# Slots, block experts and two expert loads moved around the seam between the second sequence and the expert blocks

## The chip, the cores and the metric

The kernel runs on one core of one Trainium2 chip. Its time is the device time of one execution in microseconds (us). A core has five instruction streams that run beside each other, each strictly in its own order and held up only by semaphores: PE (TensorE, matrix multiplication), DVE (VectorE), ACT (ScalarE), POOL (GpSimd) and SP (SyncE, which here only issues transfers). Transfers between the main memory and the on-chip memory (SBUF) run on 16 DMA engines; they are issued from SP, ACT or POOL. Results of PE go to eight PSUM banks.

## The reference

`x` has 8 sequences of 512 tokens with 512 channels. What is computed:

```python
xn = layernorm(x)
# attention, for each sequence, 16 heads of 32 channels
q, k, v = rotate(silu(xn @ Wq)), rotate(silu(xn @ Wk)), xn @ Wv
o = lightning_attention(q, k, v)          # decaying state, chunks of 128 tokens
o = o * sigmoid(xn @ Wg1 @ Wg2)
o = o * rsqrt(mean(o * o, per head) + 1e-6) * norm_weight
s = o @ Wo
# mixture of experts over all 4096 tokens, 16 experts, each token goes to its best 4
probs = softmax(xn @ gate_w.T)
weights, chosen = top_k(probs, 4)         # weights normalised to sum 1
mixed = sum of weights[e] * ((silu(xn @ Wg[e]) * (xn @ Wu[e])) @ Wd[e])
shared = the same with one expert for all, times sigmoid(xn @ shared_gate_w)
out = x + s * silu(mixed + shared)
```

## The kernel before

The work has three stages. **Stage one** (0 to about 316 us): all tokens are normalised, routed and run through the shared expert, the attention of sequences 0 and 1 is computed beside that, and the chosen (token, expert) pairs are sorted by expert into blocks of 128 rows. **Stage two** (to about 706 us): the expert blocks; 112 of them go as 56 pairs of one expert, the rest singly. **Stage three**: the attention of the other six sequences, and the mixture's sum, gathered per token. The change lies at the seam from stage one to stage two.

**The end of sequence 1** is the end of `sequence`, in its branch for `n == FIRST`. For each of four groups `g` of heads, `output` makes the output product `po`. Behind the last of them come: `gate_1` (the gate's first product `pg`), `squares` (the squares `sq` by ACT, their sums per head `pr` by PE, the root `rs` by ACT), `inverse` (the reciprocal of `rs` by DVE), the last quarter of the next sequence's `value` (`pv`), and `normed`: PE spreads `rs` over the channels (`pb`), and DVE multiplies it into `on`, in four instructions, one for each 128 tokens. Then `project` makes `on @ Wo` for each 128 tokens (`pw`, 8 matmuls each) and `spill` copies the result with ACT (`so`) and stores it (`s_d`).

**The table.** `table` finds which token stands at which place of which block. It is a generator: each `next(filling)` does one piece, here between the matmuls of sequence 1. It compares lists on DVE and ACT, and multiplies them on PE in four rounds of 16 matmuls (`pn`), added up by DVE in `acc`. After the last round PE folds the result (`pslot`) and DVE turns it into `slot`, the row numbers that the gathers use. The table's scratch memory is the room in `wexp` of the last `LATE` = 5 of the 16 experts. When it has been read, these experts' weights are loaded there, 768 KB each: three by SP when the last round begins (L556), the last two by ACT at the end (L1077), after `for _ in filling`, which runs the rest of the table behind everything in `sequence`.

**The block experts.** `experts_of_blocks` (six instructions by DVE, L1256 to L1263) works out from the ends of the experts' lists which expert each block belongs to, as offsets `eoff`. Its scratch is `xts`, a tile that takes the place of sequence 2's `xT`, so it waits for the last `pv`. Every block reads its weights at an offset from `eoff`, so the program cannot know which expert it touches: each read of `wexp` counts as a read of all of it, and waits for every load of `wexp` that was issued before it in the program.

**The pairs.** For each pair `j`: `gather` (POOL, two indirect DMAs that fetch the rows of 128 tokens by `slot`, into six homes, three in `xg` and three in `more`), `turn_rows` (SP, two DMA transposes of half of each row, `pl`), `transpose_x` (PE, the other half, `pt`), `join` (ACT copies `pt` and `pl` into `xts`; for pair 0 DVE copies `pl`), `prepare` (DVE copies the gate and up weights out of `wexp` into `wst`, then the routing weights `w`), `gate_up` (PE, 16 matmuls `pgu`; then `slb` by ACT and DVE), and `down` (PE, two matmuls `py` for each pair's two blocks, which read `wexp` itself; DVE scales them to `y`, SP stores `y_d`). `begin(0, ...)` starts the chain with pairs 0 and 1, with the gate's second product of sequence 2 (`gate_2`, `p` at L645, four sigmoids by ACT) between; `blocks` then goes through all pairs, turning pair j+2, preparing pair j+1 and gathering for pair j+4 around the products of pair j. `aside(j)` is a hook called in each round after `gate_up`.

**The order on an engine** is that of a scheduler which works on estimated times, except where the text pins it: `on_pe()` chains PE's instructions in program order, `behind(ENGINE)` puts an instruction behind the last one pinned on that engine, and `tc.issue_after(x)` puts one behind a given other. Four PSUM banks are called "a", two "d", one "k", one "m". The `tmp` tiles (`so`, `y`, `rs`, the gate's `g1`) share `TMP` buffers.

Of the kernel before, what the change touches and what calls it, by code (L numbers as in the profile page):

```python
# [12 lines left out]
I32 = mybir.dt.int32  # L13
U32 = mybir.dt.uint32
U16 = mybir.dt.uint16
# [19 lines left out]

NB = (B * N * TOPK + E * (P - 1)) // P
WE = KC * 2 * F + D
TMP = 4
FIRST = 2
NBQ = -(-NB // 4)  # L40

# [56 lines left out]
def tile_block(ctx: ExitStack, tc: tile.TileContext, a: dict, out: bass.AP):  # L98
# [384 lines left out]
    def table(room):  # L483
# [99 lines left out]
                    pt[h * HALF : (h + 1) * HALF, :NB], lhsT=fold,  # L583
                    rhs=acc.rearrange("p (b h) -> p b h", h=2)[:, :, h], start=True, stop=True)
        t = const.tile([P, NB], I32, tag="slot", name="slot")
        nc.vector.tensor_scalar(t, pt[:, :NB], float(B * N // 2), None, ALU.add)
        slots.append(t)


# [19 lines left out]
    def value(b, t):  # L609
        if t == 0:  # L610
            v_of[b] = att.tile([P, NC, D], F32, tag="v", name=f"v_{b}", bufs=2)
        pv = bank("d" if t % 2 else "m", f"pv_{b}_{t}")
        for k in range(KC):
            with on_pe():
                nc.tensor.matmul(  # L615
                    pv, lhsT=xT_of[b][:, k, t * P : (t + 1) * P], rhs=wv[:, k, :],
                    start=(k == 0), stop=(k == KC - 1))
            between[0]()
        nc.scalar.copy(v_of[b][:, t, :], pv)
# [4 lines left out]
    def gate_1(b):  # L624
        pg1 = bank("a", f"pg1_{b}")
        with on_pe():
            for k in range(KC):
                for t in range(NC):
                    nc.tensor.matmul(
                        pg1[t * Q : (t + 1) * Q, :P], lhsT=wg1[:, k, :],  # L630
                        rhs=xT_of[b][:, k, t * P : (t + 1) * P],
                        start=(k == 0), stop=(k == KC - 1))
        g1_of[b] = att.tile([P, P], F32, tag="tmp", name=f"g1_{b}", bufs=TMP)
        nc.scalar.copy(g1_of[b], pg1[:, :P])
# [156 lines left out]
    def inverse(b):  # L791
        nc.vector.reciprocal(rs_of[b], rs_of[b])

    def normed(b):
        pbs = [bank("a", f"pb_{b}_{c}") for c in range(NC)]
        rs = rs_of.pop(b)
        with on_pe():
            for g in range(G):
                for c in range(NC):
                    cq = slice(c * Q, c * Q + H)  # L800
                    nc.tensor.matmul(
                        pbs[c][:, g * C : (g + 1) * C], lhsT=wge[cq, g * P : (g + 1) * P],
                        rhs=rs[cq, :], start=True, stop=True)
        for c in range(NC):
            oc = on_of[b][:, :, c * C : (c + 1) * C]
            nc.vector.tensor_tensor(  # L806
                oc, oc, pbs[c].rearrange("p (g t) -> p g t", t=C), ALU.mult)

    def project(b, t):
        pw = bank("d", f"pw_{b}_{t}")  # L810
# [7 lines left out]
    def enter(b, step=lambda: None, ps=None):  # L818

        key(b, 0, ps)  # L820
        step()
        query(b, 0)
        step()
        key(b, 1)
        step()
        by_token(b, 0)
        query(b, 1)
        step()

    def sequence(b, step, projected, before=None, defer=False, also=lambda: None):  # L830


        n = b + 1

        def project_tiles(q, ts):
            if q is not None:
                for t in ts:
                    projected(q, t, project(q, t))


        fill = ([0], [1], [2], [3], [], [], [], [])
        for g in range(G):
            scores(b, g)
            step()
            if g + 2 < G:
                key(b, g + 2)
            else:
                value(n, 2 * (g - 2))
            if g + 1 < G:
                by_token(b, g + 1)  # L850
            project_tiles(before, fill[2 * g])
            step()
            if g + 2 < G:
                query(b, g + 2)
                if g + 3 == G and n not in xT_of:
                    load_xT(n)
            if g + 2 == G:
                value(n, 1)
            if g == 0 and b not in on_of:
                gate_2(b)  # L860
            project_tiles(before, fill[2 * g + 1])
            if fill[2 * g + 1] == [NC - 1]:
                on_of.pop(before, None)
            output(b, g)
            if defer and g + 2 == G:
                gate_1(n)
            step()
        v_of.pop(b)
        if n == FIRST:
            gate_1(n)  # L870
            squares(b)
            inverse(b)
            value(n, 3)
            normed(b)
            return
        if defer:
            gate_2(n)
        value(n, 3)
        also()
        squares(b)  # L880
        step()
        inverse(b)
        key(n, 0)
        also()
        query(n, 0)
        normed(b)
        also()
        if not defer:
            step()
        key(n, 1)  # L890
        by_token(n, 0)
        if defer:
            step()
        query(n, 1)
        also()
        if not defer:
            gate_1(n)
            project_tiles(b, [0, 1])
            also()
            project_tiles(b, [2, 3])  # L900
            also()
            on_of.pop(b)
        step()
# [165 lines left out]
    next(filling)  # L1069
    between[0] = lambda: next(filling, None)  # L1070
    sequence(1, lambda: None, spill)
    for _ in filling:
        pass
    between[0] = lambda: None
    slot = slots[0]
    for e in range(E - LATE // 2, E):
        nc.scalar.dma_start(wexp[:, e, :], a["experts"][:, e, :])  # L1077
    left.close()


# [4 lines left out]
    ROW = 2 * (D + E)  # L1085
    HOMES = 6
    more = att.tile([P, 2 * NC * D], U16, tag="v", name="more", bufs=2)
    homes = [blkp.tile([P, ROW], U16, tag=f"xg{j}", name=f"xg{j}") for j in range(HOMES // 2)]
    homes += [more[:, j * ROW : (j + 1) * ROW] for j in range(HOMES // 2)]
    pls = [att.tile([P, 2, KC, P], U16, tag="kT", name=f"pl{j}", bufs=2) for j in range(2)]  # L1090
    xts = att.tile([P, 2, 2, KC, P], F32, tag="xT", name="xts", bufs=1)
    wst = [
# [6 lines left out]
        {}, {}, {}, {}, {}, {}, [], [], [])  # L1099

    by_dve = [0]

    def inside(f):
        return lambda j: f(j, items[j]) if 0 <= j < len(items) else None
# [4 lines left out]
    @inside  # L1109
    def gather(j, its):  # L1110
        for i in its:
            nc.gpsimd.indirect_dma_start(  # L1112
                out=row(i), out_offset=None, in_=xn_d,
                in_offset=bass.IndirectOffsetOnAxis(ap=slot[:, i : i + 1], axis=0))

    @inside
    def turn_rows(j, its):
        for u, i in enumerate(its):
            nc.sync.dma_start_transpose(pls[j % 2][:, u], row(i)[:, D : 2 * D])

    @inside
    def transpose_x(j, its):
# [8 lines left out]
    @inside  # L1131
    def join(j, its):
        n = len(its)
        if n == 2:
            xt = xts[:, j % 2]
        else:
            xt = att.tile([P, KC, P], F32, tag="qT", name=f"xt_{its[0]}", bufs=2).unsqueeze(1)
        nc.scalar.copy(
            xt[:, :, :KP, :].rearrange("p u k t -> p u (k t)"),
            pt_of.pop(j)[:, : n * KP * P].rearrange("p (u kt) -> p u kt", u=n))  # L1140
        for u in range(n):
            (nc.vector.tensor_copy if j in by_dve else nc.scalar.copy)(  # L1142
                xt[:, u, KP:, :].bitcast(U16).rearrange("p k (t h) -> p h k t", h=2),
                pls[j % 2][:, u].rearrange("p (h k) t -> p h k t", h=2))
        xt_of[j] = xt

    def on_dve(what, i, low, high):
# [94 lines left out]
                down(j - 1)  # L1242

    def aside(j):
        if j == PAIRS:
            load_xT(FIRST)

    kept.clear()

    def experts_of_blocks():  # L1250
        half = NBQ * 2 * E
        room = xts.rearrange("p j u k t -> p (j u k t)")
        cm = room[:, :half].rearrange("p (b e) -> p b e", e=2 * E)
        ef = room[:, half : half + NBQ]
        ei = room[:, half + NBQ : half + 2 * NBQ].bitcast(I32)
        nc.vector.tensor_tensor(  # L1256
            cm, end.rearrange("p w e -> p (w e)").unsqueeze(1).to_broadcast([P, NBQ, 2 * E]),
            iota_b.unsqueeze(2).to_broadcast([P, NBQ, 2 * E]), ALU.is_le)
        nc.vector.tensor_reduce(ef, cm, axis=AX.X, op=ALU.add)
        nc.vector.tensor_copy(ei, ef)  # L1260
        nc.vector.tensor_scalar(ei, ei, E - 1, None, ALU.bitwise_and)
        nc.vector.tensor_scalar(eoff[:, 0], ei, float(WE), None, ALU.mult)
        nc.vector.tensor_scalar(eoff[:, 1], ei, float(D), None, ALU.add)  # L1263

    for j in range(3):
        gather(j)
    experts_of_blocks()
    for t in range(NC):
        spill(FIRST - 1, t, project(FIRST - 1, t))
    on_of.pop(FIRST - 1)  # L1270
    begin(0, lambda: gate_2(FIRST, banks="aakd"))
    by_dve.clear()
    blocks(range(len(items) + 2), aside)
# [4 lines left out]
    with tc.If(count > SURE):  # L1278
        items[:] = [(i,) for i in range(SURE, NB)]
        done.clear()  # L1280
        gone.clear()
        for j in range(3):
            gather(j)
        begin(0)
        blocks(range(len(items) + 2))
# [177 lines left out]
```

## Time and profile before

| | |
|---|---|
| Three runs | 1148.9, 1152.95 and 1152.28 us, median 1152.28 |
| Profiled execution | 1155.04 us, of which the span from first to last instruction is 1153.2 us |
| Busy, share of the span | PE 97%, DVE 64%, POOL 39%, ACT 37% |
| Mean granted clock of TensorE | 0.990 |
| PE idle in all | about 35 us |
| One pair of blocks, in the middle of stage two | 5.61 us, PE without a gap |

The profile is of one execution. "PE" lines of the timeline give start and duration in us, the line of the code, the operation with its output and inputs, and the number of instructions in a group; a bracket at the end says how long the engine had been idle before and whose end released it. Matmuls overlap a little, so the distance of two starts is the better measure of what one costs. The granted clock is the share of full speed at which TensorE was allowed to run; it is given for any stretch of time.

### The profile page before, as it was taken

How to read it: one execution, taken by the hardware profiler on the slowest of the kernel's cores; microseconds unless marked ns; L12 is line 12 of the kernel's file. 1: busy time of each engine (PE TensorE's matmuls, PEld its weight loads, DVE VectorE, ACT ScalarE, POOL GpSimd, SP SyncE). 2: the span in 40 equal slices, each digit the busy share in tenths (PEclk: the TensorE clock that was granted, in tenths of full speed). 3: DMA queues.
4: the chain of work that ended last, by engine and by line, in shares of the span. 5: the costliest groups of instructions: out<-in, count | busy, mean ns of one | idle time of the engine just before them, and what ended most of it. 6: DMA issues, size and time to landing. Idle time of an engine off the chain costs nothing. (4 is left out here: it accounts for less than half of the span.)

```text
span 1153.2 us, 21330 instructions
## 1 busy us (share of the span) xinstructions
PE 1117.9 (97%) x7670; PEld 679.7 (59%) x7670; DVE 736.7 (64%) x1580; ACT 429.3 (37%) x927; POOL 446.8 (39%) x427
## 2 busy tenths in 40 slices
PE   7999999989899999999999999999999999999998
PEld 4445554445477777777777775555645545545554
DVE  6358734899334444555444445968879597697784
ACT  3223424154253333333333342353351522522541
POOL 3213100300233333333333322764877857958211
PEclk9999999989999999999999999999999999999999
DMA  9975431191799999999999994833737637434012
GB/s 338 319 276 194 156 127 47 51 352 40 217 200 236 220 244 238 238 241 237 253 233 234 272 215 178 323 101 108 254 116 230 183 108 244 150 122 145 29 36 75
DMA packets 163931, 218.49 MB, mean 189 GB/s; under 512 B 89840, under 2 KB 99184, under 8 KB 161776
## 3 DMA queue, kind: packets, MB, share of 16 engines
q1 hardware_dynamic: 142416, 145.18, 40.5%
q0 software_dynamic: 21120, 70.34, 23.9%
q10 hardware_dynamic: 288, 1.57, 0.4%
q8 instruction: 63, 1.03, 0.4%
q14 instruction: 44, 0.36, 0.1%
HBM read 126.78 MB, written 72.43 MB: 173 GB/s over the span
## 5 line engine op out<-in xcount | busy, mean ns | idle before, releaser
L1180 PE MATMUL pgu<-xts,wst 128*128 128x256 f32 x896 | 204.3, 381 | 0.0
L1180 PEld LDWEIGHTS pgu<-xts,wst 128*128 128x128 f32 x896 | 171.3, 191 | 46.7 <-issue 13.4
L1112 POOL DMA_INDIRECT xg<-xn_d,slot x69 | 65.7, 953 | 229.4 <-DVE w L1163 118.4
L1313 POOL DMA_INDIRECT yg<-y_d,place x128 | 142.5, 1113 | 31.1 <-issue 18.5
L1215 DVE TENSOR_SCALAR y<-py,w 128x512 f32<-128x512 f32 x136 | 101.6, 750 | 44.7 <-PE py L1211 31.0
L1211 PE MATMUL py<-wexp,slb 128*128 x272 | 129.9, 593 | 0.0
L615 PE MATMUL pv<-wv,xT 128*128 128x512 f32 x256 | 120.1, 610 | 3.1 <-DMA xT<-xT_d 2.0
L659 PE MATMUL pq<-xT,wq 128*128 128x512 f32 x256 | 118.2, 604 | 0.3 <-PEq L1278 0.3
L659 PE MATMUL pk<-xT,wk 128*128 128x512 f32 x256 | 118.2, 603 | 0.0
L1192 ACT ACTIVATE slb<-pgu 128x256 f32<-128x256 f32 (+1 forms) x80 | 28.1, 351 | 222.5 <-PE pgu L1180 184.1
L813 PE MATMUL pw<-wo,on 128*128 128x512 f32 x224 | 103.9, 612 | 5.8 <-DVE m L1351 5.8
L1193 DVE TENSOR_TENSOR slb<-slb,pgu 128x256 f32<-128x256 f32 (+1 forms) x80 | 30.5, 381 | 119.5 <-ACT slb L1192 118.1
L1112 POOL DMA_INDIRECT more<-xn_d,slot x67 | 63.5, 948 | 93.1 <-DVE w L1163 56.9
L1355 POOL TENSOR_TENSOR xo<-xo,m 128x512 f32<-128x512 f32 x31 | 45.3, 1460 | 131.2 <-DVE m L1351 123.3
L1142 ACT COPY xts<-pl 128x512 uint16<-128x512 uint16 x110 | 84.1, 767 | 9.0 <-DMA pl<-xg 9.0
L659 PEld LDWEIGHTS pq<-xT,wq 128*128 128x128 f32 x256 | 48.1, 193 | 55.3 <-issue 53.9
L748 DVE TENSOR_TENSOR sc<-ps,dmask 128x512 f32<-128x512 f32 x128 | 79.0, 676 | 0.9 <-PE ps L723 0.9
L615 PEld LDWEIGHTS pv<-wv,xT 128*128 128x128 f32 x256 | 46.3, 191 | 53.7 <-issue 47.1
L813 PEld LDWEIGHTS pw<-wo,on 128*128 128x128 f32 x224 | 42.5, 196 | 57.1 <-issue 47.7
L659 PEld LDWEIGHTS pk<-xT,wk 128*128 128x128 f32 x256 | 46.2, 189 | 50.7 <-issue 48.3
L1161 DVE COPY wst<-wexp 128x512 f32 x112 | 42.8, 424 | 39.8 <-DVE y L1215 18.7
L1211 PEld LDWEIGHTS py<-wexp,slb 128*128 128x128 f32 x272 | 45.5, 191 | 27.4 <-issue 26.8
(196 smaller groups left out, 1716.5 us busy)
## 6 DMA issues: line engine op xcount, KB each, us to landing
y_d<-y SPq DMA_DIRECT2D x136, 256.0 KB
wexp<-in_experts SPq DMA_DIRECT2D x14, 768.0 KB
sh_d<-sh SPq DMA_DIRECT2D x32, 256.0 KB
xT<-xT_d SPq DMA_DIRECT2D x8, 1024.0 KB
m<-sh_d SPq DMA_DIRECT2D x32, 256.0 KB
xo<-in_x SPq DMA_DIRECT2D x32, 256.0 KB
out<-xo SPq DMA_DIRECT2D x31, 256.0 KB
x<-in_x SPq DMA_DIRECT2D x7, 1024.0 KB
```

Of the source, the lines that this page charges most:

```text
L615: nc.tensor.matmul(pv, lhsT=xT_of[b][:, k, t * P : (t + 1) * P], rhs=wv[:, k, :], start=(k == 0), stop=(k == KC - 1))
L659: nc.tensor.matmul(ps, lhsT=w[:, k, g * P : (g + 1) * P], rhs=xT_of[b][:, k, :], start=(k == 0), stop=(k == KC - 1))
L748: nc.vector.tensor_tensor(s, pss[j].rearrange("p (c t) -> p c t", t=C), dmask[:, g * HG + j].unsqueeze(1).to_broadcast([P, NC, C]), ALU.mult)
L813: nc.tensor.matmul(pw, lhsT=on_of[b][:, g, t * P : (t + 1) * P], rhs=wo[:, g, :], start=(g == 0), stop=(g == G - 1))
L1112: nc.gpsimd.indirect_dma_start(out=row(i), out_offset=None, in_=xn_d, in_offset=bass.IndirectOffsetOnAxis(ap=slot[:, i : i + 1], axis=0))
L1142: (nc.vector.tensor_copy if j in by_dve else nc.scalar.copy)(xt[:, u, KP:, :].bitcast(U16).rearrange("p k (t h) -> p h k t", h=2), pls[j % ...
L1161: nc.vector.tensor_copy(to, wflat[:, bass.ds(off + u * KC * F, KC * F)])
L1180: nc.tensor.matmul(pg[:, o * 2 * P : (o + 1) * 2 * P], lhsT=wst[j % 2][k // KP][:, (k % KP * 2 + o) * F :][:, :F], rhs=xt[:, :, k, :], sta ...
L1211: nc.tensor.matmul(py, lhsT=hT[:, u * P : (u + 1) * P], rhs=wflat[:, bass.ds(off + KC * 2 * F, D)], start=True, stop=True)
L1215: gone.append(nc.vector.tensor_scalar(y, py, w[:, u : u + 1], None, ALU.mult).ins)
L1313: nc.gpsimd.indirect_dma_start(out=yg, out_offset=None, in_=y_d, in_offset=bass.IndirectOffsetOnAxis(ap=place[:, r, g : g + 1], axis=0))
L1355: nc.gpsimd.tensor_tensor(xo, xo, m, ALU.add)
```

## The change

- **The table's end** moves: its last pieces run directly behind sequence 1's last output product, ahead of `gate_1` and `squares`, so `slot` is made there and the gathers have it.
- **`experts_of_blocks`** moves up, from beside the projection to directly behind the reciprocal and ahead of `value` and `normed`; its scratch is now the room of the last two experts in `wexp`.
- **The last two expert loads** move from ACT, after the table, to SP, in the rounds `j` = 1 and `j` = 3 of the pairs.
- **Homes**: the first three gathers go to `more`, the next three to `xg`.
- **Buffers**: `TMP` goes from 4 to 5.
- **Pins**: `slot`, the block experts, the gathers, the `pl` copies and the row transposes are pinned in program order on their engines; the weights' first `wst` copy is put behind the last `on` product (`gone += scaled`).

```diff
-TMP = 4
+TMP = 5
...
-        nc.vector.tensor_scalar(t, pt[:, :NB], float(B * N // 2), None, ALU.add)
+        with behind(DVE):
+            nc.vector.tensor_scalar(t, pt[:, :NB], float(B * N // 2), None, ALU.add)
...
-            nc.vector.tensor_tensor(
-                oc, oc, pbs[c].rearrange("p (g t) -> p g t", t=C), ALU.mult)
+            scaled[:] = [nc.vector.tensor_tensor(
+                oc, oc, pbs[c].rearrange("p (g t) -> p g t", t=C), ALU.mult).ins]
...
+    def experts_of_blocks():
+        half = NBQ * 2 * E
+        room = wflat[:, (E - LATE // 2) * WE :]
...
         if n == FIRST:
+            for _ in range(4):
+                next(filling)
             gate_1(n)
+            next(filling, None)
             squares(b)
             inverse(b)
+            experts_of_blocks()
             value(n, 3)
             normed(b)
             return
...
     sequence(1, lambda: None, spill)
-    for _ in filling:
-        pass
     between[0] = lambda: None
     slot = slots[0]
-    for e in range(E - LATE // 2, E):
-        nc.scalar.dma_start(wexp[:, e, :], a["experts"][:, e, :])
...
-    homes = [blkp.tile([P, ROW], U16, tag=f"xg{j}", name=f"xg{j}") for j in range(HOMES // 2)]
-    homes += [more[:, j * ROW : (j + 1) * ROW] for j in range(HOMES // 2)]
+    homes = [more[:, j * ROW : (j + 1) * ROW] for j in range(HOMES // 2)]
+    homes += [blkp.tile([P, ROW], U16, tag=f"xg{j}", name=f"xg{j}") for j in range(HOMES // 2)]
...
         for u, i in enumerate(its):
-            nc.sync.dma_start_transpose(pls[j % 2][:, u], row(i)[:, D : 2 * D])
+            with tc.issue_after(turned[-1]) if turned else nullcontext():
+                turned.append(nc.sync.dma_start_transpose(
+                    pls[j % 2][:, u], row(i)[:, D : 2 * D]).ins)
...
         for u in range(n):
-            (nc.vector.tensor_copy if j in by_dve else nc.scalar.copy)(
+            with behind(DVE if j in by_dve else ACT):
+                (nc.vector.tensor_copy if j in by_dve else nc.scalar.copy)(
...
     def aside(j):
+        if j in (1, 3):
+            e = E - LATE // 2 + j // 2
+            nc.sync.dma_start(wexp[:, e, :], a["experts"][:, e, :])
         if j == PAIRS:
             load_xT(FIRST)
...
-    def experts_of_blocks():
-        half = NBQ * 2 * E
-        room = xts.rearrange("p j u k t -> p (j u k t)")
...
     for j in range(3):
         gather(j)
-    experts_of_blocks()
     for t in range(NC):
         spill(FIRST - 1, t, project(FIRST - 1, t))
     on_of.pop(FIRST - 1)
+    gone += scaled
     begin(0, lambda: gate_2(FIRST, banks="aakd"))
```

The order of the compiled instructions differs only at this seam, except for ACT's copies in the pairs: in every pair it now copies `pt` and then both `pl`, where before it copied one `pl`, `pt`, and the other `pl`. On SP the first of the two loads stands behind the row transposes of pair 3 and ahead of those of pair 4; the second stands behind the stores of blocks 0 to 3 and the transposes of pairs 5 and 6 that were issued by then. The first `py` of pair 0 waits for the first load, that of pair 2 for the second; so do DVE's `wst` copies for pairs 3 and 5. On ACT all four `so` copies now stand ahead of the pairs' first copies.

## The prediction

> **What bounds the kernel now.** I read the page's busy times first, then PE's waits, the timeline of the seam, and the granted clock there.
>
> ```profile
> PE 1117.9 (97%) x7670; PEld 679.7 (59%) x7670; DVE 736.7 (64%) x1580; ACT 429.3 (37%) x927; POOL 446.8 (39%) x427
> ...
> PE pslot L582 <- DVE on L806: 2.8, 1, 2.8
> PE pv L615 <- DMA xT<-xT_d: 2.0, 1, 2.0
> PE p L645 <- ACT so L996: 1.9, 1, 1.9
> ```
>
> The first line is the page's busy time; the others are from the list of PE's waits (total, times, longest, in us). PE bounds nearly everywhere, so only PE's 35 us of idle time, and time in which PE is slow, can be won. Two of these waits, `pslot` and `p`, lie in the change's reach, 4.7 us together; the `pv` between them stands elsewhere. PE's timeline there:
>
> ```profile
> 291.55 0.42 PE L784 MATMUL pr<-sq,sel 128*32 128x128 f32 x8 [0.25 <-ACT sq L781]
> 291.91 2.84 PE L615 MATMUL pv<-wv,xT 128*128 128x512 f32 x6
> 294.68 1.23 PE L566 MATMUL pn<-wexp 128*64 128x286 f16 x16
> 295.84 1.12 PE L615 MATMUL pv<-wv,xT 128*128 128x512 f32 x2
> 296.89 1.17 PE L801 MATMUL pb<-rs,wge 16*128 16x128 f32 x32
> 300.83 0.26 PE L582 MATMUL pslot<-wexp 128*64 128x143 f16 x2 [2.76 <-DVE on L806]
> 301.01 15.67 PE L813 MATMUL pw<-wo,on 128*128 128x512 f32 x32
> ...
> 319.88 1.15 PE L645 MATMUL p<-g,wg 32*128 32x128 f32 x26 [1.90 <-ACT so L996]
> 320.97 5.41 PE L1180 MATMUL pgu<-xts,wst 128*128 128x256 f32 x16
> ...
> 326.65 3.62 PE L1180 MATMUL pgu<-xts,wst 128*128 128x256 f32 x16
> ```
>
> The projection `pw` starts late, and the first `pgu` takes 5.41 us where the next, of the same shape, takes 3.62. Why the second is so is seen in stretches of the clock (PE busy first, the granted clock third from the end):
>
> ```profile
> 297.60:301.00 3.40, 0.64 (x21) 0.49 (x14) 3.30 (x6) 0.58 (x1) 0.00 (x0) 1.00 0.51 166
> 301.00:304.40 3.40, 3.40 (x6) 1.51 (x5) 1.96 (x6) 0.00 (x0) 0.72 (x1) 0.50 0.81 295
> 318.00:321.40 3.40, 1.52 (x28) 1.37 (x29) 0.00 (x0) 3.37 (x7) 2.49 (x4) 1.00 1.06 225
> 321.50:324.90 3.40, 3.40 (x9) 2.70 (x8) 0.00 (x0) 3.37 (x6) 0.41 (x1) 0.50 1.60 298
> ```
>
> Each stretch in which PE was under half busy is followed by one of the same length at half clock, which costs half of it, 1.7 us. So two short waits cost 2.8 + 1.9 us and another 3.4 us behind them.
>
> **What the change takes off.**
>
> 1. *The wait before `pw`.* Last comes DVE:
>
> ```profile
> 293.21 0.95 DVE L792 RECIPROCAL rs<-rs 128x128 f32<-128x128 f32 x1 [3.24 <-ACT rs L788]
> 297.00 1.36 DVE L1256 TENSOR_TENSOR xts<-end,iota_b 128x1152 f32<-128x1152 f32 x1 [0.60 <-PE pv L615]
> 300.09 2.47 DVE L806 TENSOR_TENSOR on<-on,pb 128x512 f32<-128x512 f32 x4
> ```
>
> The block experts stand ahead of `on` and waited for the last `pv`, since they write in that tile's place. In `wexp` they need not. The same work from 288.95, where the last `po` ends, in the new order by distances of starts: `pn` 1.16, `pg` 0.88, `pslot` 0.18, `pr` 1.83 (its 0.25 wait falls away: `sq` is done by then), so `pr` ends at 293.0. `rs` 0.37, reciprocal 0.95: 294.4. Four of the block experts took 3.18 (297.00 to 300.18), the last two 0.25: 297.8. The first `on` (a quarter of 2.47) ends at 298.45, and `pw` can start at 298.6. PE's own work up to there (`pv` 3.82, `pb` 1.17) ends at 298.0. So `pw` starts 2.4 us earlier. Bounds: 3.0 (all idle gone, 0.25 + 2.76) and 1.5 (the root's table load on ACT, which took 1.28 and ended at 292.8, slides by 0.9 with its neighbours).
>
> 2. *The half clock in `pw`.* With 0.6 us idle no stretch is under half busy: 1.7 won. Bounds 0 and 1.7.
>
> 3. *The wait in `p`.* In the trace ACT ran two `pl` copies, held for 7.53 us by the transposes, before the last `so` copies. Now all `so` stand first, and the gathers start at about 292.5 instead of 303.68: 1.9 won. Bounds 1.5 (if the last `so` follows `pw` by its 0.58) and 1.9.
>
> 4. *The half clock in the first `pgu`*: 5.41 − 3.62 = 1.8 won. Bounds 0 and 1.8.
>
> The sum is 7.8 us. DVE's 2.17 us wait for the last expert load (305.13) goes too, worth nothing: PE is in `pw` until 316.5. Taking ACT's two issues away (2.34 + 0.33 us) is worth nothing either: the `v` copy behind them waited for PE. The fifth `tmp` buffer, ACT's copy order (in mid-stage ACT idles 3.46 us in each pair) and the homes' order cost and win nothing by these rows, 0.3 either way.
>
> The Trainium skill, "TensorE: Matmul & The Clock Gate", section "Part 1: The HAM clock gate", speaks of a free-running window of 3413 ns, which fits the stretches, but puts the half clock behind a whole idle window. By that rule waits of 2.8 and 1.9 us would not bring it, and points 2 and 4 would be worth nothing (4.3 in all). The rows above have it twice behind windows that were 19% and 45% busy, so I go by them.
>
> **What it puts in.** The two loads, 1.57 MB, had landed at about 305 under `pw`. Now `py` of pair 0 waits for the first, `py` of pair 2 for the second, and PE stands in order behind each.
>
> 5. *The first load.* Need: the first `pgu` starts at 320.97 − 2.4 − 1.7 − 1.9 = 315.0, ends at 318.4; `pt` 0.44; the second `pgu` 3.45, held perhaps 0.3 by the sigmoid that frees its bank (ACT: `so`, two `pt`, two `pl`, a table load, three sigmoids, end near 319); `pt` 0.44. So `py` is due at 323.1. Issue: SP reaches it behind pair 3's transposes. Those need POOL's gathers behind the first `pt` (now about 313.4); the trace's gathers at 317.17 and 318.47 let SP's transposes go at 320.8 and 323.1, 3.6 and 4.6 later, so now at about 317.2 and 319.5, each 1.2 to 2.1 of SP. It waits as well for `wst` of pair 2, behind the first `pgu`: 319.3. Issue 320.7 (319.4 to 321.7). Landing: the three loads by SP at L556, issued at 287.41, took 6.3 us from first to last packet with the queues else empty, 2.1 each, and began 1.0 after issue. In the pairs other traffic keeps the engines full: the trace moved 263 GB/s in 320 to 325, 61 in 325 to 330, 210 in 330 to 335. At some 235 GB/s 0.79 MB is 3.4 us: landed at 325.1, a wait of 2.0. Best: 319.4 + 1.0 + 2.1 = 322.5, none. Worst: half of 210 GB/s, 7.5 us, behind issue at 321.7: 330.2, 7 us. I take 2.3, nearer the middle rows since gathers and transposes share the way, and behind it one half-clock stretch, 1.7, as behind the 1.90 wait.
>
> 6. *The second load.* It is issued behind the stores of pair 1's two `y`. From the end of pair 1's `py`: the last `y` 0.8, two store issues 1.0, start 1.0, 3.4 of data: 6.2. PE has a `pgu` (3.45), `pt` (0.44) and half a `pgu` (1.7) meanwhile: 5.6. With the stores' 0.5 MB ahead in part, I take 1.0; bounds 0 and 4.
>
> 7. DVE's `wst` copies of pairs 3 and 5 wait for these loads too, with `w` and so POOL's later gathers queued behind. Their `pgu` comes a pair later than the `py` that waits anyway: 0; bound 2, if gathers fall behind. The bank of the second `pgu`: 0.3.
>
> Given back: 2.3 + 1.7 + 1.0 + 0.3 = 5.3. Left: 7.8 − 5.3 = 2.5 us faster. From there on the pairs run in the old rhythm (PE without idle at 5.61 us) and the rest has the same order, so it reaches the end. Against the profiled execution's 1155.04 that is 1152.5. That execution lies 2.8 above the median of 1152.28; I put the same 2.5 against the median: **1149.8 us**.
>
> The skill's "DMA: Bandwidth & Descriptors", section "Two DMAs through the same engine are not ordered", says that within one queue of one engine descriptors start in order. That speaks against this change: ACT's loads had a queue of their own, and SP's stand behind its transposes and stores. If pair 3's transposes drain first and both stores before the second load, some 2 us each, points 5 and 6 would come to 4.3 and 3.0, and the gain to nothing (−1.5). No row shows a large load behind transposes, so this stays in the range.
>
> **Rivals.**
>
> *A. The loads hide.* SP issues early and the gathers' earlier start leaves the engines idle: no stall, at most 0.3 given back. 1152.28 − 7.5 = 1144.8. For it: the gathers begin 11 us earlier, so pairs 0 to 2 are done before the first `pgu`. Against: pair 3's gathers depend on the first `pt` and go just then.
>
> *B. Slower: the first load lands late.* Its place is `py` of pair 0; the price is the wait plus its half-clock stretches, and it turns the sign when both loads' waits pass about 6 us. At the worst end, 7 and 4 us with two stretches (3.4) and late gathers (2): 16.4 − 7.8, or 8.6 slower, 1160.9; halfway, 4.5 slower, 1156.8. For it: the 61 GB/s stretch. Against: such stretches are mostly one or two us long elsewhere in the pairs.
>
> *C. The change does not do what it says*: ACT's chain (`so`, `pt`, `pl`, sigmoids) holds the second `pgu` and the clock stays halved, leaving only 2.4 of the gain and the loads' waits: 2.4 − 3.3 = about 1 slower, 1153.
>
> **How the numbers follow.** Measurement tells some 0.5%, 5.8 us, from no change. Forecast (some of the gain eaten) 0.48, A 0.26, B 0.16, C 0.10. The forecast's own range is 1146 to 1153. Faster by over 0.5% (under 1146.5) is A and a little of the forecast: 0.28. Slower by over 0.5% (over 1158) is the late half of B and some unseen cost in the pairs: 0.13. Same: 0.59. The range takes A's 1144.8 with a microsecond below, and B's middle: 1143.5 to 1157.
>
> **What would show it.** `pw` starts under 10 us after the last `po` ends (12.1 before); no half-clock stretch in `pw`; the first `pgu` at 3.6; POOL's first gather near 292.5; then a wait of PE in the list of waits at `py` for a DMA of `wexp`, 2 to 4 us in all, and a half-clock stretch behind it. No such wait means A; over 6 us B. Wrong altogether would be a changed rhythm in the pairs (not 5.61 us).

## The result and the profile after

The changed kernel takes 1163.4 us (1159.63 to 1165.96), the kernel before 1152.47 in the same comparison: ratio 1.0096, 95% interval 1.0067 to 1.0126. That is 11 us slower; the forecast was 2.5 faster, with a range up to 1157. The profiled execution took 1165.96, its span 1164.1 (before: 1155.04 and 1153.2).

The page's busy line, and the list of PE's waits (total, times, longest):

```profile
PE 1118.8 (96%) x7670; PEld 679.2 (58%) x7670; DVE 738.2 (63%) x1580; ACT 435.1 (37%) x927; POOL 446.2 (38%) x427
...
PE pgu L1215 <- ACT xt L1171: 7.9, 5, 2.6
...
PE py L1240 <- DMA wexp<-in_experts: 6.8, 2, 3.6
...
PE pw L816 <- DVE on L809: 1.3, 1, 1.3
```

PE does the same work. The waits of `pslot` (2.8) and `p` (1.9) are gone; 1.3 us before `pw` is left of them. In their place are two new ones: `py` for the two expert loads, which was forecast at 3.3 us, and one that was not forecast at all, `pgu` of the single blocks (L1215) for `xt`. PE's timeline shows both in place:

```profile
296.76 14.00 PE L816 MATMUL pw<-wo,on 128*128 128x512 f32 x32 [1.34 <-DVE on L809]
...
312.87 3.69 PE L1209 MATMUL pgu<-xts,wst 128*128 128x256 f32 x16
...
316.84 3.62 PE L1209 MATMUL pgu<-xts,wst 128*128 128x256 f32 x16
...
324.46 2.79 PE L1240 MATMUL py<-wexp,slb 128*128 x4 [3.57 <-DMA wexp<-in_experts]
327.05 4.52 PE L1209 MATMUL pgu<-xts,wst 128*128 128x256 f32 x16
...
342.61 3.62 PE L1240 MATMUL py<-wexp,slb 128*128 x4 [3.27 <-DMA wexp<-in_experts]
...
635.57 1.89 PE L1215 MATMUL pgu<-wexp,xt 128*128 x8
...
647.00 1.13 PE L1215 MATMUL pgu<-wexp,xt 128*128 x4 [1.76 <-ACT xt L1171]
...
698.08 2.08 PE L1215 MATMUL pgu<-wexp,xt 128*128 x4 [2.64 <-ACT xt L1171]
...
716.81 1.02 PE L660 MATMUL pk<-xT,wk 128*128 128x512 f32 x2
```

The same places before:

```profile
330.54 1.88 PE L1211 MATMUL py<-wexp,slb 128*128 x4
...
634.72 1.89 PE L1186 MATMUL pgu<-wexp,xt 128*128 x8
...
705.10 1.02 PE L659 MATMUL pk<-xT,wk 128*128 128x512 f32 x2
```

The seam did what the change set out to do. `pw` runs at full clock (14.00 us, before 15.67), the first `pgu` too (3.69, before 5.41), and the second `pgu` starts at 316.84 instead of 326.65: 9.8 us ahead, of which 1.7 only because everything up to the last `po` lay earlier in this execution. Then it is lost. Against the kernel before, PE stands 6.1 ahead when the first `py` starts (324.46 against 330.54), and 0.9 behind at the first single block's `pgu` (635.57 against 634.72). Of these 10.7 us the two waits (3.57 and 3.27) and what half clock adds to the `py` and `pgu` behind them (2.79 and 3.62 against 1.88, 4.52 against 3.62: 3.55) make up 10.4. The single blocks, from there to the first `pk` of stage three, take 81.2 us instead of 70.4. That is another 10.8, and stage three is as before (447.3 and 448.1 us). The waits bring half clock with them, as before (stretches of the clock: busy PE first, granted clock third from the end):

```profile
321.90:325.30 3.40, 0.84 (x2) 0.49 (x3) 0.00 (x0) 0.94 (x2) 0.00 (x0) 1.00 1.15 311
325.30:328.70 3.40, 3.40 (x7) 1.94 (x6) 1.70 (x3) 0.00 (x0) 0.00 (x0) 0.52 0.41 117
339.00:342.40 3.40, 0.34 (x2) 0.00 (x0) 0.00 (x0) 0.57 (x1) 0.00 (x0) 1.00 0.94 370
342.40:345.80 3.40, 3.19 (x4) 1.52 (x5) 0.75 (x1) 0.00 (x0) 0.00 (x0) 0.52 0.39 80
694.00:697.40 3.40, 1.44 (x6) 0.74 (x4) 0.00 (x0) 0.13 (x1) 0.00 (x0) 1.00 1.09 169
697.40:700.80 3.40, 2.72 (x8) 2.26 (x9) 1.50 (x5) 2.19 (x6) 0.00 (x0) 0.51 0.59 189
```

**Where the single blocks lose.** ACT's timeline where pairs give way to single blocks, before:

```profile
626.73 0.77 ACT L1142 COPY xt<-pl 128x512 uint16<-128x512 uint16 x1 [2.60 <-PE pgu L1180]
627.59 0.38 ACT L1192 ACTIVATE slb<-pgu 128x256 f32<-128x256 f32 x1
627.87 0.37 ACT L1138 COPY xt<-pt 128x256 f32<-128x256 f32 x1
628.64 0.76 ACT L1142 COPY xt<-pl 128x512 uint16<-128x512 uint16 x1 [0.40 <-DMA pl<-more]
632.98 0.38 ACT L1192 ACTIVATE slb<-pgu 128x256 f32<-128x256 f32 x1 [3.58 <-PE pgu L1180]
633.26 0.37 ACT L1138 COPY xt<-pt 128x256 f32<-128x256 f32 x1
```

and after:

```profile
628.45 0.38 ACT L1221 ACTIVATE slb<-pgu 128x256 f32<-128x256 f32 x1 [3.24 <-PE pgu L1209]
628.73 0.37 ACT L1166 COPY xt<-pt 128x256 f32<-128x256 f32 x1
628.98 0.78 ACT L1171 COPY xt<-pl 128x512 uint16<-128x512 uint16 x1
633.84 0.38 ACT L1221 ACTIVATE slb<-pgu 128x256 f32<-128x256 f32 x1 [4.08 <-PE pgu L1209]
634.12 0.37 ACT L1166 COPY xt<-pt 128x256 f32<-128x256 f32 x1
634.37 0.78 ACT L1171 COPY xt<-pl 128x512 uint16<-128x512 uint16 x1
```

The copy of `pl` for block 113 ran at 628.64, 4.6 us ahead of its `pt` copy, as soon as its transfer had landed. The change pins `pl` behind `pt` (`behind(ACT)` in `join`), so it runs at 634.37. Only then is that `pl` buffer free for block 115's row transpose, which SP now issues behind sequence 2's 1 MB `xT` load and two stores of `y`. So the order on SP differs here too; the text on the change named ACT's copies alone. SP's timeline before (the transposes of blocks 114 and 115, then the `xT` load):

```profile
627.52 3.09 SPq L1119 DMA_TRANSPOSE pl<-xg  x2
...
632.97 0.32 SPq L597 DMA_DIRECT2D xT<-xT_d  x1
```

and after:

```profile
633.83 0.32 SPq L598 DMA_DIRECT2D xT<-xT_d  x1
635.70 1.18 SPq L1245 DMA_DIRECT2D y_d<-y  x2
636.98 3.33 SPq L1146 DMA_TRANSPOSE pl<-more  x2
```

Before, the two transposes were issued at 627.52 and 629.43; after the change block 115's, the first of the last two here, goes at 636.98. From there on it seems to echo: block 115's home is free for block 121's gather only when the transpose has read it. POOL issued that gather at 646.93 (before 641.39), block 127's at 666.03 (659.68), block 133's at 685.57 (677.17).

### The profile page after: what moved, and what is told of

It is laid out like the page before. It is cut to its first block, busy times and chain, and to the rows that moved or that the text cites. A ratio compares the mean times of both kernels' runs of the same rounds, so it can differ in the third digit from the quotient of the medians.

```text
span 1164.1 us, 21329 instructions
## 1 busy us (share of the span) xinstructions
PE 1118.8 (96%) x7670; PEld 679.2 (58%) x7670; DVE 738.2 (63%) x1580; ACT 435.1 (37%) x927; POOL 446.2 (38%) x427
## 5 line engine op out<-in xcount | busy, mean ns | idle before, releaser
L1138 POOL DMA_INDIRECT more<-xn_d,slot x69 | 66.0, 956 | 232.5 <-DVE w L1192 98.6
L1240 PE MATMUL py<-wexp,slb 128*128 x272 | 132.8, 604 | 6.8 <-DMA wexp<-in_experts 6.8
L1138 POOL DMA_INDIRECT xg<-xn_d,slot x67 | 63.3, 945 | 101.8 <-DVE w L1192 56.6
L1171 ACT COPY xts<-pl 128x512 uint16<-128x512 uint16 x110 | 76.6, 767 | 0.0
```

What stands on the lines that cost most here:

```text
L1138: nc.gpsimd.indirect_dma_start(out=row(i), out_offset=None, in_=xn_d, in_offset=bass.IndirectOffsetOnAxis(ap=slot[:, i : i + 1], axis=0))
L1171: (nc.vector.tensor_copy if j in by_dve else nc.scalar.copy)(xt[:, u, KP:, :].bitcast(U16).rearrange("p k (t h) -> p h k t", h=2), pls[j % ...
L1240: nc.tensor.matmul(py, lhsT=hT[:, u * P : (u + 1) * P], rhs=wflat[:, bass.ds(off + KC * 2 * F, D)], start=True, stop=True)
```

## The experiments

My theory after the profile: two independent causes, the late loads (some 10 us with the half clock behind them) and the pin on ACT's copies (5 to 11). Rivals: the waits in the single blocks come from other edits or from the transfers' shifted phase, and something else at the seam takes the loads' place.

**First four, on another chip.** Experiment 1 takes the pin away; 2 has ACT issue the two loads ahead of the projection, as before; 3 does both; 4 puts the pin alone into the kernel before.

```diff
 # 1 and 3
-            with behind(DVE if j in by_dve else ACT):
+            with behind(DVE) if j in by_dve else nullcontext():
 # 2 and 3
+    for e in range(E - LATE // 2, E):
+        nc.scalar.dma_start(wexp[:, e, :], a["experts"][:, e, :])
     left.close()
...
-        if j in (1, 3):
-            e = E - LATE // 2 + j // 2
-            nc.sync.dma_start(wexp[:, e, :], a["experts"][:, e, :])
 # 4, in the kernel before
+            with nullcontext() if j in by_dve else behind(ACT):
```

> The changed kernel with one pin taken away: ACT's copies of pl stand again where the scheduler puts them (DVE's stay pinned). On SP the row transpose of block 115 goes back ahead of the 1 MB load of sequence 2's xT. Theory (the pin makes the waits in the single blocks): PE's waits for xt in the single blocks, 7.9 us, and the half-clock stretch behind them, 1.7, go; the waits for the two expert loads stay. Time about 10 below the changed kernel, near 1153. Rival (the waits come from the other edits there, the chained transposes or the turned order of homes, or from the shifted phase of the transfers): 7.9 us of waits stay, 1163.

> The changed kernel, but ACT issues the last two expert loads right behind the block experts, ahead of the projection, as before the change. Theory (the seam loses what it won to the loads alone): the waits of py for wexp, 6.8 us, and the two half-clock stretches behind them, 3.5, go, no other wait takes their place, and the first single block begins about 9.8 us earlier than before the change; the single blocks keep their waits. Time about 10.5 below the changed kernel, near 1153. Rival (ACT's chain or the gathers of pairs 3 to 5 hold PE instead): half of it or less comes back, 1158 or more.

> Both edits together: early loads by ACT, no pin on ACT's pl copies. Theory: the two causes are independent and add, so about 20 to 21 below the changed kernel and 9 to 10 below the kernel before, 1142 to 1144. Rival (a kernel that reaches the single blocks earlier runs into late transfers there anyway): 1148 to 1153.

> The kernel before with one edit of the change alone: ACT's pl copies pinned behind pt. Theory: the seam stays as before the change, the single blocks get waits for xt of some 8 us and a half-clock stretch: about 1162. Rival (it needs the rest of the change): 1152.

Measured, as ratios to before (1164.45 on this chip): 1.0059 (1.0038 to 1.0080), 1.0052 (1.0024 to 1.0079), 1.0000 (0.9977 to 1.0022) and 1.0062 (1.0032 to 1.0093). The expected times were missed, since this chip is slower for the kernel before too, and the changed kernel was not among the four. The single blocks tell the pin's part: 71.0 and 70.4 us without it (1, 3), 76.4 and 73.0 with it (2, 4; the stretch of experiment 2 has 4.9 us of waits for `xt`). The pin alone costs the old kernel 0.6%. But experiment 3 only equals the kernel before. ACT's timeline in experiment 2, which has the same loads, shows one reason:

```profile
288.24 4.04 ACTq L1103 DMA_DIRECT2D wexp<-in_experts  x1
292.31 1.28 ACT L789 ACT_TABLE_LOAD   x1 [3.92 <-issue]
293.61 0.37 ACT L789 ACTIVATE rs<-pr,eps_rms 128x128 f32<-128x128 f32 x1
```

The scheduler put the first load's issue ahead of the root `rs`, and it held ACT for 4.0 us; reciprocal, `on` and `pw` slid with it (`pw` at 298.9, half clock in it). Besides, the second `pgu` waited 3.1 us for the sigmoids in both (the last section comes back to this). So 2 and 3 undo part of what the change won, and don't price the loads.

**The changed kernel again, before again, and cleaner edits.** Experiment 7 pins only the first six pairs, so the seam's order stays that of the changed kernel; 8 also moves the loads early, but on SP (the diff of 2 with `nc.sync`), so ACT is left alone.

```diff
-            with behind(DVE if j in by_dve else ACT):
+            with behind(DVE if j in by_dve else ACT) if j < 6 else nullcontext():
```

> The changed kernel itself, again, beside runs of the kernel before on the same chip, since the first four experiments ran on a chip on which the kernel before takes 12 us longer, mostly in the third stage. Theory (the loads cost the seam its gain, the pin costs some 8 to 11 in the single blocks): ratio to before near 1.009 again, the single blocks (first single pgu to stage three) take 5 to 11 longer than the 70.4 of the kernel before. Rival (the waits in the single blocks were an accident of one execution): ratio near 1.000.

> The kernel before, as a kernel of its own, for its profile on this chip and for what the comparison calls no difference: ratio 1.000. Both theories expect the single blocks to take 70 to 71 us with no wait for xt.

> The changed kernel with ACT's pl copies pinned in the first six pairs only, so the seam keeps the order of the changed kernel on every engine and only ACT's copies from pair 6 on, and the place of block 115's transpose on SP, go back. Theory: the waits for xt in the single blocks vanish (70 to 71 us for that stretch), the waits of py for the two loads stay; 8 to 11 below the changed kernel. Rival: they stay because the kernel's transfers reach that place in another phase.

> As the last, and the two expert loads issued by SP ahead of the projection: the first behind the table's last read, the second behind the block experts. In the second and third experiment ACT's issue of the first load stood ahead of the root of rs and held it (4.0 us of issue), so that pw began late; here nothing on ACT moves. Theory: pw begins as in the changed kernel, the waits of py for wexp and the half clock behind them go (10 us), the first single block begins 9 to 10 earlier than before the change: 8 to 10 below the kernel before. Rival (ACT's chain or slow table loads hold the second pgu): 2 to 5 below it.

Measured: 1.0092 (1.0065 to 1.0119), 0.9990 (0.9970 to 1.0009), 1.0045 (1.0020 to 1.0071), 0.9935 (0.9914 to 0.9956). The single blocks took 72.7, 70.4, 71.3 and 70.4 us. So the loss repeats; undoing the pin wins 5.9 us, less than the 8 to 11 expected; and with both undone the seam's gain shows: 1144.25 against 1152.72, within the 8 to 10 expected. In the profile of the fifth the single blocks lost only 2.3 us, where 5 to 11 were expected, and the waits of `py` more (6.9, and 4.7 that the list puts down to a `pl` transfer, though the first load's last packet came 1.3 before PE started): the two parts' sizes vary between executions.

**Why the loads are late, and why the pin hurts.** Experiment 9 has ACT issue the loads in the same rounds of pairs, so they have a queue of their own. Experiment 10 puts the `xT` load behind block 116's transpose. Experiment 11 has early loads by SP with the pin everywhere.

```diff
 # 9
-            nc.sync.dma_start(wexp[:, e, :], a["experts"][:, e, :])
+            nc.scalar.dma_start(wexp[:, e, :], a["experts"][:, e, :])
 # 10
-        if j == PAIRS:
-            load_xT(FIRST)
+        if j == PAIRS + 2:
+            with tc.issue_after(turned[-1]):
+                load_xT(FIRST)
```

> The changed kernel with the two loads still in the rounds of pairs 1 and 3, but issued by ACT, so they have a queue of their own and do not stand behind SP's transposes and stores. Theory A (in SP's queue they wait their turn: 2.3 to 2.9 us from issue to the first packet, against 1.0 with an empty queue): first packet about 1.0 to 1.5 after issue, each wait of py about 1.5 to 2 shorter (ACT comes to the first issue some 2 us later, which takes that back there), so 2 to 4 below the changed kernel. Theory B (what holds them is the share of the 16 engines): first packet as late, or the 0.79 MB takes longer than the 2.3 to 5 us seen; the same time as the changed kernel within 2 us.

> The changed kernel with the 1 MB load of sequence 2's xT put behind block 116's transpose on SP, ACT's pins kept. It separates two ways in which the pin can hurt the single blocks. Theory A (block 115's transpose stands behind that load in SP's queue): the waits for xt in the single blocks fall to 0 to 2 us, the time is 4 to 6 below the changed kernel. Theory B (the pin alone, pl copied only behind pt, leaves one buffer too few in flight): the waits stay at 2 to 8 us and the time too.

> The changed kernel with the loads issued early by SP and the pin kept everywhere, to price the pin without waits for loads. Theory: as the eighth experiment up to the single blocks, which take 73 to 81 us instead of 70.4: ratio to before 0.996 to 1.003, 3 to 11 above the eighth. Rival (the pin hurts only with what the late loads leave behind): like the eighth, ratio 0.9935.

Measured on yet another chip (before 1164.4): 1.0069 (1.0041 to 1.0097), 1.0120 (1.0067 to 1.0173), 1.0001 (0.9972 to 1.0030).

Experiment 9: from issue to the first packet the loads took 1.0 and 1.8 us. Issued by SP they took 2.75 and 1.85 in the first profile, and 1.4 to 3.3 over all profiles of kernels with SP's late loads (1.4 and 2.4 on this chip, in experiment 10). The data then took 2.7 and 5.4 us, much as by SP (2.3 to 3.7 for the first, 3.0 to 6.1 for the second), against 2.1 to 2.9 for the loads of L556, just ahead of the gathers. By this one profile both theories hold a part: some tenths of a us to 2 us of the queue, and up to 3 us of sharing. What it saves in time isn't settled, as the changed kernel did not run on that chip.

Experiment 10 fells its theory A. The `xT` load was out of the way, and PE waited 5.7 us for `xt` all the same, in single blocks that took 80.4 us:

```profile
PE py L1240 <- DMA wexp<-in_experts: 8.0, 1, 8.0
...
PE pgu L1215 <- ACT xt L1171: 5.7, 5, 3.6
```

So it is not that one load. What is left is the pin itself, that a copy of `pl` can't run ahead of its `pt`. How the delay then goes round the homes is read from the profile, not shown by a run of its own.

Experiment 11 has no wait for a load, and single blocks of 72.5 us; it lies where theory put it, but on a chip where the fourth corner was missing. So the last four runs put all four corners on one chip.

**Two by two.**

> The changed kernel, both parts in: late loads and pin. Theory: ratio to before 1.009 as on the first chip, 1.010 to 1.015 on one with slow table loads. Rival (the chip decides): near 1.000 on such a chip.

> Late loads, pin in the first six pairs only. Theory: the parts add, so 5 to 6 us below the changed kernel (the pin's share), single blocks 70 to 71 us. Rival (the pin matters only by accident): within 2 us of the changed kernel.

> Early loads by SP, pin everywhere. Theory: 12 to 14 us below the changed kernel (the loads' share with the half clock behind them), no wait of py for wexp, single blocks 72 to 81. Rival (another wait takes the loads' place): 6 or less below it.

> Early loads by SP, pin in the first pairs only. Theory: the two shares add, 18 to 20 below the changed kernel, ratio to before 0.993 on a chip like the first, 0.994 to 0.998 where table loads are slow, since the second pgu then waits some 3 us for the sigmoids. Rival (the shares overlap, the same slack pays for both): 13 or less below the changed kernel.

| before 1151.59 | pin everywhere | pin in the first pairs |
|---|---|---|
| loads late, in the pairs | 1161.01 (ratio 1.0080, 1.0053 to 1.0107) | 1156.49 (1.0034, 1.0014 to 1.0055) |
| loads early, by SP | 1149.07 (0.9972, 0.9951 to 0.9993) | 1144.42 (0.9930, 0.9902 to 0.9957) |

The loads cost 11.9 and 12.1 us, the pin 4.5 and 4.7: they add. By the intervals in the table each of these differences is uncertain by some 4 us (an estimate), so that they add holds no closer than that. The expectations lay a little higher: 5 to 6 us for the pin, 12 to 14 for the loads and 18 to 20 for both, against 4.5, 11.9 and 16.6. Without both the kernel is 7.2 us faster than before. Neither load was moved alone, and the change's other edits (the homes, the fifth buffer, the chained transposes) are in all four corners. PE's waits in the execution with neither, whose list has no wait of 0.5 us or more at the seam or in the blocks but the 1.3 before `pw`:

```profile
PE psT L286 <- DMA ident<-in_ident: 6.7, 1, 6.7
PE pw L816 <- DVE m L1368: 4.4, 4, 1.9
PE pk L692 <- DVE state L739: 4.2, 1, 4.2
PE pv L616 <- DMA xT<-xT_d: 2.1, 1, 2.1
PE pw L816 <- DVE on L809: 1.3, 1, 1.3
```

Its first single block starts at 627.4 (before 634.7), and its `py` of pair 0 at 323.21 without a wait:

```profile
322.78 0.60 PE L1156 MATMUL pt<-ident,more 128*128 128x128 f32 x4
323.21 1.88 PE L1242 MATMUL py<-wexp,slb 128*128 x4
```

In the four profiles the waits of `py` for the loads are 7.8, 11.3, none and none; those of the single blocks for `xt` 3.7, none, 4.8 and 0.3.

## Why the prediction was wrong

*Points 1 to 4, the seam's gain: right in the sum.* 7.8 us forecast; 7.2 and 8.5 measured with both causes of loss out (experiments 15 and 8). `pw` started 9.5 us behind the `pn` that follows the last `po` directly (287.25; before, 12.1 behind the end of `po`), with no half-clock stretch in it or in the first `pgu`, and POOL's first gather went at 290.33. The rows of half clock behind short waits were the right ones to go by: the rule of a whole idle window in the Trainium skill ("TensorE: Matmul & The Clock Gate", "Part 1: The HAM clock gate") would have left 4.3, and here again a stretch that was 25% busy (0.84 of 3.40) and one 42% busy (1.44) were followed by half clock. But "under half busy" is no sure sign of it: in experiment 12 a stretch 43% busy (1.47 of 3.41) was followed by full clock. In the second profile of the kernel before (experiment 6) the wait in `p` was 1.5 us, the stretch around it 55% busy (1.88 of 3.41), and the first `pgu` took 3.72 at full clock. So the 1.8 us of point 4 were not lost in every execution, and no run prices the four points one by one.

*Points 5 and 6, the loads: the mechanism right, the sizes not.* 5.0 forecast with the half clock, 12.0 measured. In the terms of the sum, with SP's timeline after:

```profile
318.05 0.53 SPq L1276 DMA_DIRECT2D wexp<-in_experts  x1
...
333.37 2.64 SPq L1146 DMA_TRANSPOSE pl<-more  x2
336.07 1.04 SPq L1245 DMA_DIRECT2D y_d<-y  x2
337.22 0.40 SPq L1276 DMA_DIRECT2D wexp<-in_experts  x1
```

- PE was due at the first load's `py` at 320.9, not 323.1, but SP issued the load at 318.05, not 320.7: these two nearly cancel. The data took 2.6 and 3.1 us, a little less than the 3.4 of the sum.
- "Start 1.0" came from loads in an empty queue. Behind transposes and stores it was 2.75 and 1.85. That fits what the Trainium skill says of order within one queue ("DMA: Bandwidth & Descriptors", "Two DMAs through the same engine are not ordered"), which the forecast left in the range. With it the waits would have been 4.3 and 3.0, near the 3.57 and 3.27 of this profile.
- The second load was taken to be issued 1.8 us behind the end of pair 1's `py`. It was 3.7 (337.22 against 333.56): pair 6's two transposes, waiting for their gathers, stand ahead of the stores on SP, and the working never priced them.
- From the last packet to PE's start there was 1.05 us for the first load (323.41 to 324.46) and 0.44 for the second, which had no term. What fills it is not shown.
- Each load brought its half-clock stretch, not only the first: 1.7 us more behind the second (`py` 3.62 against 1.88). And the waits vary: in the profiles of the two corners with late loads they came to 7.8 and 11.3, against 6.8 here.

*"ACT's copy order ... cost and win nothing by these rows, 0.3 either way": wrong: the pin on that order cost 4.5 and 4.7 us (2.2 to 10.8 in the single blocks of single profiles).* The row was ACT's idle time in the middle of the pairs, where no copy of `pl` waited for its transfer (none from 400 to 600 us, before or after) and PE loses nothing. It was carried over to the single blocks without reading their rows. There ACT waited for `pl` already before the change (2.11 us at 647.66), the copies of blocks 112 and 113 ran ahead of their turn, and the pin forbids just that. With it fell the sentence "the rest has the same order, so it reaches the end".

*Rivals.* B had the place and the sign, but its price stopped at the loads. "What would show it" did name the waits at `py`, and their 6.8 us pointed to B; it gave the pairs' rhythm as the sign of something else, and that rhythm stayed at 5.61.

## What to carry to other kernels

A load moved off a quiet stretch is priced with what stands ahead of it in its queue, on the issuing engine and on the DMA engines, and with the time from landing to the waiter; durations from an empty queue are only a lower bound. A pin that fixes an order is a change everywhere that line runs: look for the stage where the pinned operation runs ahead of its neighbour, since that lead is what it takes away. And when a change has several parts, build the corners: here the version with two of its edits taken back, the loads' place and the pin beyond the first pairs, beats both kernels.

## What was not expected of the hardware

- Chips seem to differ. The kernel before took 1151.6 to 1152.7 us on three occasions and 1164.4 on two others. Every occasion whose chip is on record was on a chip of its own, so the chip is the likely cause, not a shown one. In the slower profiles stage three was longer (455 to 460 us from its first `pk`, 447 to 448 in the first two profiles), and ACT's table load at the seam came 3.2 to 4.9 us late in the six kernels there that have the changed seam, with nothing in the profile holding it; in experiment 1:

```profile
320.18 1.28 ACT L650 ACT_TABLE_LOAD   x1 [3.21 <-issue]
```

  where the changed kernel's own profile has no gap before that load. In those six the second `pgu` waits 1.5 to 3.2 us for the sigmoids.
- The issue of one 768 KB load held ACT for 4.04 us in experiment 2, where SP's loads were still under way; before the change the two issues took 2.34 and 0.33, and the first of these began 1.6 us behind the last packet of SP's loads. What holds ACT there is not shown.
